# Whole or four-way split projections on TensorE: choosing the tile shape by the neighbouring pieces

## Chip, cores and metric

The kernel runs on one core of a Trainium2 chip. The metric is the device time of one execution in microseconds (us). The core has a matrix engine (TensorE, PE in the profile, with its weight loads shown apart as PEld), VectorE (DVE), ScalarE (ACT), GpSimd (POOL), and a queue on SyncE (SP) that issues most DMAs.

## The reference

One block of a recurrent model (RWKV) in float32, on 8 sequences of 256 tokens with 512 channels:

```python
xn = _ln(x, ln1_w, ln1_b); sx = _token_shift(xn, state[:, i1])
xxx = jnp.tanh((xn + sx * maa_x) @ maa_w1).reshape(b, l, 5, 1, 32)
xxx = jnp.matmul(xxx, maa_w2).reshape(b, l, 5, E)
x5 = xn[:, :, None] + sx[:, :, None] * (maa_stack + xxx)          # five mixes
w = jnp.exp(-jnp.exp(time_decay + jnp.tanh(x5[:, :, 1] @ decay_w1) @ decay_w2))
r, k, v = x5[:, :, 3] @ Wr.T, x5[:, :, 0] @ Wk.T, x5[:, :, 2] @ Wv.T
g = jax.nn.silu(x5[:, :, 4] @ Wg.T)
# scan over 256 steps, 32 heads of 16 channels:
#   a = k_t v_t;  out = r_t (u * a + s);  s = a + w_t * s
att = group_norm(outs) * gn_w + gn_b
x = x + att * g @ Wo.T
# feed-forward part: layer norm, token shift, two mixes, then
rr = jax.nn.sigmoid(xr @ ffn_Wr.T); kk = jnp.square(jax.nn.relu(xk @ ffn_Wk.T))
x = x + rr * (kk @ ffn_Wv.T)
```

## The kernel before

The work of one sequence is cut into pieces, each a few instructions of one engine, and into three stages: `inputs_of_scan` (layer norm, mixes, the projections to w, k, v, r, g), `scan` (the recurrence, as scans along time on VectorE over channel pairs, with sums on TensorE) and `rest` (group norm, output projection, feed-forward part). Stages of neighbouring sequences run at the same time.

The order is fixed before anything is emitted. `Plan.sequence` gives each piece a rank out of a long written table (`TURNS`). `Plan.order` then takes, again and again, the piece of lowest rank whose predecessors have been taken, and gives it a planned start from assumed costs (`LATENCY`, `SWITCH`, `GAP`, and the time in each piece). The order on each engine comes from the ranks, the dependencies and from which buffers are held. The planned times decide one more thing: which buffer of a pool a piece gets (the one freed last among those free at its planned start). On the chip each engine runs its pieces in that order and waits on semaphores.

The pieces of TensorE, with their lines:

- `project` (L576): 128 output channels of a projection, four contraction steps of a 128x128 weight tile against 256 tokens. `project_tokens` (L591): half a projection with tokens as the output rows, two steps against 512 channels. The same shape of work at L606, L701, L896 and, with 128 columns, L472. All of these use the whole 128x128 array; the planner calls that mode `full`.
- Transposes (L530), also on the whole array.
- Column pieces, which give each instruction 32 output columns, four of them side by side: `gather` (L793, sums of the scan, 16 matmuls), L735 and L819 (4 matmuls each). L658 (the decay and fifth-mix inputs) uses two tiles of 64 columns.
- Row pieces: L626 (32 rows), L673 and L834 (64 rows).

One matmul in float32 stands in the profile as two MATMUL instructions, each with its LDWEIGHTS. So a `project` piece is 8 MATMUL rows, a `project_tokens` piece 4, a `gather` 32.

Other lines that the text speaks of: L361 issues DMAs, L780 (multiply), L782 (scan) on VectorE and L785 on GpSimd are the recurrence, L648 and L859 are additions and products on GpSimd.

Of the kernel before, what the change touches and what calls it, by code (L numbers as in the profile page):

```python
# [58 lines left out]
class Op:  # L59
    def __init__(self, engine, us, outs, ins, emit, mode):  # L60
        self.engine, self.us, self.emit, self.mode = engine, us, emit, mode
        self.bufs = list(dict.fromkeys([*outs, *ins]))
        self.before, self.after, self.waits = [], [], 0
        self.ready = self.start = self.end = 0.0
        self.number, self.kind = 0, engine + "".join(c for c in self.bufs[0].name if not c.isdigit())


class Plan:
# [186 lines left out]
    def order(self, phases):  # L255
# [7 lines left out]
        while queue:  # L263
# [6 lines left out]
            at = max([at] + [sorted(s[0] for s in self.pools[p])[n - 1] for p, n in need.items()])  # L270
# [5 lines left out]
            if op.mode and op.mode != mode[op.engine]:  # L276
                at += self.SWITCH[op.engine]
                mode[op.engine] = op.mode
            for b in op.bufs:
# [18 lines left out]
            for o in op.after:  # L298
                same = o.engine == op.engine and op.lag < 1 and not op.wire
                o.ready = max(o.ready, op.end + self.GAP[op.engine] if same else landed + op.lag)  # L300
# [6 lines left out]
        self.span = max(op.end for op in done)  # L307
        return sorted(done, key=lambda op: op.start)


@with_exitstack
def tile_rwkv_block(
# [50 lines left out]

    def pe(us, outs, ins, emit, mode="full", into=()):
        plan.add("PE", us, outs, ins, emit, mode, into)

    def act(n, out, ins, emit, table=None, pointers=0):
        plan.add("ACT", 0.1 + n * 0.00084 + 0.09 * pointers, [out], ins, emit, table)

    def dve(n, outs, ins, emit, each=1.05):  # L370
        plan.add("DVE", 0.083 + n * each / 1e3, outs, ins, emit)

# [87 lines left out]
    def centered_weights():  # L460
# [5 lines left out]
        for k in range(NK):  # L466
            ps, w = new("ps", f"psW{k}"), wvs[k]
            for half in range(2):

                def mm(k=k, ps=ps, half=half):  # L470
                    for n in range(2):
                        nc.tensor.matmul(  # L472
                            ps()[:, half, n * P : (n + 1) * P], lhsT=raw[2 * half + n]()[:, k * P : (k + 1) * P],
                            rhs=cen()[:, 0, 0:P], start=True, stop=True)
# [10 lines left out]
    def normed(src, which, row, b, alone=False):  # L485
# [5 lines left out]
        if (which == 1 and b > 1) or (which == 2 and (b < 5)):  # L491
# [8 lines left out]
            gp(2, rs, [mv], lambda: nc.gpsimd.tensor_scalar(  # L500
                rs(), mv()[:, :, 1], 1.0 / E, EPS, ALU.mult, ALU.add), 30)
        else:
# [5 lines left out]
            act(2, mn, [mv], lambda: nc.scalar.mul(mn(), mv()[:, :, 0], -1.0))  # L508
            gp(2, rs, [mv, eh], lambda: nc.gpsimd.tensor_tensor(rs(), mv()[:, :, 1], eh()[:, 0:2], ALU.add), 30)
        gp(2, rs, [rs, eh], lambda: nc.gpsimd.tensor_tensor(rs(), rs(), eh()[:, 2:4], ALU.pow), 310)  # L510
        gp(2, nm, [mn, rs], lambda: nc.gpsimd.tensor_tensor(nm(), mn(), rs(), ALU.mult), 30)
        for n in range(NT):
# [7 lines left out]
            xh.append(t)  # L520
        xns, sxs = [], []
        i = NVEC + 2 * b + row
        for q in range(NQ):
# [7 lines left out]

            pe(0.55, [ps], [*xh, idt], turn, into=[xn])
            act(2, xn, [vec, ps], lambda q=q, xn=xn: nc.scalar.copy(xn()[:, :, 0:1], vec()[:, 2 * q : 2 * q + 2, i : i + 1]))
# [34 lines left out]
    def project(w, src, q, name, into):  # L568

        ps = new("ps", name)  # L570
        for m in range(2):
            o = (2 * q + m) * P

            def mm(m=m, o=o):
                for k in range(NK):
                    nc.tensor.matmul(  # L576
                        ps()[:, m, :], lhsT=w[k]()[:, o : o + P], rhs=src[k // 2]()[:, k % 2, :],
                        start=(k == 0), stop=(k == NK - 1),
                    )

            pe(1.73, [ps], [*w, *src], mm, into=[into])
        return ps

    def project_tokens(w, src, n, name, into):

        ps = new("ps", name)
        for h in range(2):

            def mm(h=h):
                for k in (2 * h, 2 * h + 1):  # L590
                    nc.tensor.matmul(  # L591
                        ps().rearrange("p m t -> p (m t)"), lhsT=src[h]()[:, k % 2, n * P : (n + 1) * P], rhs=w[k](),
                        start=(k == 0), stop=(k == NK - 1),
                    )

# [3 lines left out]
    def inputs_of_scan(b, got):  # L599
# [4 lines left out]
        def mm():  # L604
            for k in range(NK):
                nc.tensor.matmul(  # L606
                    px()[:, 0, :], lhsT=w1()[:, k, 0:P], rhs=xin[k // 2]()[:, k % 2, :], start=(k == 0), stop=(k == NK - 1))

        pe(1.73, [px], [w1, *xin], mm, into=[ta])
        act(256, ta, [px], lambda: nc.scalar.activation(ta(), px()[:, 0, :], AF.Tanh), "exp")  # L610

        def mixed(pair):
# [7 lines left out]
            for lot in lots:  # L620
# [9 lines left out]

                pe(0.97, [ps[g, q] for g, q, *_ in lot], [tb, w2b] if pair == (4,) else [ta, w2a], mm, "rows32", [x5[g][q] for g, q, *_ in lot])
                for g, q, *_ in lot:
# [28 lines left out]
        pe(1.73, [pd], [dw1, w1, *x5[1], *xin], mm, "columns64", [hd, tb])  # L661
        for rows in (slice(0, 64), slice(64, 128)):
# [12 lines left out]

        pe(0.97, pw, [dw2, hd], mm, "rows64", ws)
        for q in range(NQ):
# [14 lines left out]
        if b == 0:  # L692
# [3 lines left out]
            for m in range(2):  # L696
                ps, vo = new("ps", f"psv{b}_0_{m}"), new("vo", f"vo{b}_0_{m}")

                def mm(m=m, ps=ps):
                    for k in range(NK):  # L700
                        nc.tensor.matmul(  # L701
                            ps()[:, m, :], lhsT=vs_[k]()[:, m * P : (m + 1) * P], rhs=x5[2][k // 2]()[:, k % 2, :],
                            start=(k == 0), stop=(k == NK - 1))

                pe(1.73, [ps], [*vs_, *x5[2]], mm, into=[t])
                act(256, t, [ps], lambda m=m, t=t, ps=ps: nc.scalar.copy(t()[:, m, 1 : T + 1], ps()[:, m, :]))
# [13 lines left out]
    def scan(b, got):  # L720
# [17 lines left out]
        atts = [new("att", f"att{b}_{q}") for q in range(NQ)]  # L738
        pe(0.47, [pc], [hm, *rks], mm, "columns")
        for q in range(NQ):  # L740
# [4 lines left out]
        for blk in range(NK):  # L745
# [20 lines left out]
            for i in range(4):  # L766
# [9 lines left out]
                if i == 3 and ((b == 0 and blk) or (b == 1 and blk < 3)):  # L776
                    gp(4 * T, vs, [vs, k], lambda m=m, vs=vs, k=k: nc.gpsimd.tensor_tensor(
                        vs(), vs(), k.place[:, m : m + 1, 1 : T + 1].to_broadcast([P, 4, T]), ALU.mult))
                else:
# [3 lines left out]
                    st().rearrange("p n t -> p (n t)"), w().rearrange("p n t -> p (n t)"),  # L783
                    vs().rearrange("p n t -> p (n t)"), 0.0, ALU.mult, ALU.add), 2.06)
                gp(4 * T, st, [st, r], lambda m=m, st=st, r=r: nc.gpsimd.tensor_tensor(  # L785
                    st(), st(), r()[:, m : m + 1, :].to_broadcast([P, 4, T]), ALU.mult))
                done.append(st)
# [9 lines left out]

            pe(1.83, [pat], [con, *done], gather, "columns")
            dve(256, [att], [pat, att], lambda m=m, att=att, pat=pat: nc.vector.tensor_tensor(  # L799
# [5 lines left out]
    def rest(b, got):  # L805
# [16 lines left out]

        pe(0.47, [pv], [con, *sqs], mm, "columns")
        act(256, rs, [pv, eh], lambda: nc.scalar.activation(
            rs()[:, 0:T], pv()[:, 0, :], AF.Sqrt, bias=eh()[:, 0:1]), "sqrt", 1)
        dve(256, [rs], [rs], lambda: nc.vector.reciprocal(rs()[:, 0:T], rs()[:, 0:T]), 6.25)
        if last:
# [8 lines left out]

            pe(0.97, pr, [con, rs], mm, "rows64")
        ys = []
# [48 lines left out]
        for n in range(NT):  # L887
            o, t = os[n], x2[n]
            if last and n:
                for h in range(2):  # L890
# [3 lines left out]
                    def mm(ps=ps, n=n, cols=cols):  # L894
                        for k in range(NK):
                            nc.tensor.matmul(  # L896
                                ps()[:, 0, :], lhsT=kk[k // 2]()[:, k % 2, n * P : (n + 1) * P],
                                rhs=Wfv[k]()[:, cols], start=(k == 0), stop=(k == NK - 1))

# [20 lines left out]
    load(w2a, maa_w2[0:4].rearrange("g j e -> (g j) e"), 256)  # L920
    load(w2b, maa_w2[4:6].rearrange("g j e -> (g j) e"), 128)
    load(dw1, decay_w1.rearrange("(k p) j -> p k j", p=P), 128)
# [12 lines left out]
    with tc.manual_schedule():  # L935
        for op in plan.order(phases):
            op.emit()

# [73 lines left out]
```

## Time and profile before

| | us |
|---|---|
| Median of 3 runs (629.31 to 632.11) | 631.82 |
| The profiled execution | 631.53 |
| Its span, first to last instruction | 629.7 |
| TensorE busy, 3568 MATMULs | 608.1 |
| VectorE busy | 544.8 |
| GpSimd busy | 521.8 |
| ScalarE busy | 467.5 |

The profiled execution takes 1.8 us more than its span. The granted TensorE clock is 0.999 of full speed. Ends of matmuls are modelled in the profile, so the times between starts are what can be read closely: the duration of a row overlaps with the start of the next one.

### The profile page before, as it was taken

To read this page: it belongs to the slowest core of one execution; us is meant where nothing else is said; L and a number is where in the kernel's file an instruction comes from. 1 tells how busy PE (TensorE), PEld (TensorE's weight loads), DVE (VectorE), ACT (ScalarE), POOL (GpSimd) and SP (SyncE) were. 2 spreads that over 40 slices of the span, in tenths; PEclk is the share of its full clock that TensorE was granted. 3 is DMA by queue.
4 is the path that set the end of the run, shared out by engine and by line. 5 is a ranking of instruction groups with operands and counts; after the bars stand their busy time and mean duration, and the time that the engine had idled before them with its cause. 6 is when DMAs were issued, how large, how long until landed. Compare 5 with 4: busy or idle time off the path is not lost.

```text
span 629.7 us, 10253 instructions
## 1 busy us (share of the span) xinstructions
PE 608.1 (97%) x3568; PEld 408.6 (65%) x3568; DVE 544.8 (87%) x471; ACT 467.5 (74%) x1045; POOL 521.8 (83%) x420
## 2 busy tenths in 40 slices
PE   5899999999999999999999999999999999899997
PEld 4687777768555776477664776576765677556464
DVE  5689999999999999888997999899999999895331
ACT  2777869779977789788879798877887585776431
POOL 2699999899997999889888899999688989788040
PEclk9999999999999999999999999999999999999999
DMA  8697867597857877877778589598769886962541
GB/s 287 201 243 224 204 179 178 152 256 200 235 161 201 238 174 219 252 210 199 191 192 246 158 238 262 143 253 228 216 173 237 229 218 165 243 212 82 209 140 71
DMA packets 57778, 127.84 MB, mean 203 GB/s; under 512 B 7616, under 2 KB 16576, under 8 KB 57728
## 3 DMA queue, kind: packets, MB, share of 16 engines
q1 hardware_dynamic: 53360, 123.00, 72.3%
q10 hardware_dynamic: 4368, 4.20, 2.1%
q8 instruction: 28, 0.46, 0.3%
q14 instruction: 22, 0.18, 0.1%
HBM read 115.11 MB, written 8.39 MB: 196 GB/s over the span
## 4 chain that ended last, share of the span: by engine, by line
PE 64%; POOL 9%; DVE 8%; ACT 7%; DMA 6%; SPq 3%; issue 3%; ACTq 0%; POOLq 0%; DVEq 0%
PE ps L576 29%; PE ps L591 19%; PE ps L793 5%; DMA vs<-vo 5%; DVE st L782 4%; POOL st L785 4%; SPq L361 3%; PE ps L626 3%; PE ps L530 2%; PE ps L606 2%; PE ps L658 1%; POOL g L859 1%; DVE vs L780 1%; PE ps L673 1%; ACT xh L518 1%
## 5 line engine op out<-in xcount | busy, mean ns | idle before, releaser
L782 DVE TENSOR_TENSOR_SCAN st<-wrep,vs 128x1024 f32<-128x1024 f32 x128 | 289.4, 2279 | 6.3 <-ACT wrep L763 3.4
L785 POOL TENSOR_TENSOR st<-st,r 128x1024 f32<-128x1024 f32 x128 | 254.5, 2001 | 14.3 <-DVE st L782 13.8
L780 DVE TENSOR_TENSOR vs<-vs,ps 128x1024 f32<-128x1024 f32 x122 | 144.3, 1206 | 5.7 <-ACT vs L773 5.6
L591 PE MATMUL ps<-Ws,mix 128*128 128x512 f32 x248 | 112.3, 598 | 0.8 <-ACT o L883 0.8
L648 POOL TENSOR_TENSOR mix<-mix,xn 128x512 f32<-128x512 f32 x78 | 84.9, 1100 | 9.5 <-DVE mix L642 5.1
L591 PEld LDWEIGHTS ps<-Ws,mix 128*128 128x128 f32 x248 | 45.7, 190 | 53.3 <-issue 47.1
L636 ACT ACTIVATE ps<-ps,vec 128x256 f32<-128x256 f32 x140 | 59.5, 444 | 16.5 <-PE ps L626 14.6
L793 PE MATMUL ps<-st,con 128*32 128x256 f32 x1024 | 62.5, 382 | 0.9 <-POOL st L785 0.9
L576 PE MATMUL ps<-mix,Wr 128*128 128x256 f32 x256 | 60.7, 382 | 0.0
L576 PE MATMUL ps<-mix,Wg 128*128 128x256 f32 x256 | 60.7, 383 | 0.0
L576 PE MATMUL ps<-mix,Wk 128*128 128x256 f32 x256 | 60.3, 381 | 0.0
L591 PE MATMUL ps<-Ws,g 128*128 128x512 f32 x128 | 57.4, 599 | 2.8 <-POOL g L859 2.8
L576 PE MATMUL ps<-mix,Ws 128*128 128x256 f32 x256 | 59.3, 383 | 0.0
L576 PE MATMUL ps<-mix,Wv 128*128 128x256 f32 x240 | 56.6, 382 | 1.3 <-DVE att L799 0.9
L576 PEld LDWEIGHTS ps<-mix,Wg 128*128 128x128 f32 x256 | 47.6, 190 | 11.8 <-issue 5.0
L576 PEld LDWEIGHTS ps<-mix,Ws 128*128 128x128 f32 x256 | 47.7, 190 | 11.0 <-issue 3.8
L576 PEld LDWEIGHTS ps<-mix,Wk 128*128 128x128 f32 x256 | 47.8, 190 | 9.6 <-issue 3.4
L638 DVE TENSOR_TENSOR mix<-ps,sx 128x512 f32<-128x512 f32 x70 | 46.3, 680 | 8.9 <-ACT ps L636 7.6
L576 PEld LDWEIGHTS ps<-mix,Wr 128*128 128x128 f32 x256 | 47.5, 190 | 9.1 <-issue 1.7
L576 PEld LDWEIGHTS ps<-mix,Wv 128*128 128x128 f32 x240 | 44.9, 190 | 12.3 <-issue 3.1
L563 POOL TENSOR_TENSOR mix<-mix,xn 128x512 f32<-128x512 f32 x44 | 47.7, 1098 | 3.0 <-ACT mix L561 2.8
L773 ACT ACTIVATE vs<-s,cm 128x4 f32<-128x4 f32 x128 | 35.9, 295 | 18.5 <-DMA vs<-vo 17.2
(114 smaller groups left out, 902.7 us busy)
## 6 DMA issues: line engine op xcount, KB each, us to landing
vs<-vo SPq DMA_DIRECT2D x128, 512.0 KB, 5.5
Ws<-in_fr SPq DMA_DIRECT2D x16, 512.0 KB, 5.5
Ws<-in_wo SPq DMA_DIRECT2D x16, 512.0 KB, 4.9
Ws<-in_fk SPq DMA_DIRECT2D x16, 512.0 KB, 5.9
Ws<-in_fv SPq DMA_DIRECT2D x16, 512.0 KB, 4.6
x<-in_x SPq DMA_DIRECT2D x9, 512.0 KB, 5.6
vo<-v ACTq DMA_DIRECT2D x15, 256.0 KB, 2.7
out<-o SPq DMA_DIRECT2D x15, 256.0 KB, 3.7
```

What stands on the lines that cost most here:

```text
L361: plan.add("DMA", 0.6, [out] if out else [], [src] if src else [], lambda: nc.sync.dma_start(out=dst(), in_=in_()), lag=lag, kb=kb, part=part)
L563: gp(512, t, [t, xn[q]], lambda q=q, t=t: nc.gpsimd.tensor_tensor(t(), t(), xn[q]()[:, :, 1 : T + 1], ALU.add))
L576: nc.tensor.matmul(ps()[:, m, :], lhsT=w[k]()[:, o : o + P], rhs=src[k // 2]()[:, k % 2, :], start=(k == 0), stop=(k == NK - 1),)
L591: nc.tensor.matmul(ps().rearrange("p m t -> p (m t)"), lhsT=src[h]()[:, k % 2, n * P : (n + 1) * P], rhs=w[k](), start=(k == 0), stop=(k = ...
L636: act(256, p_, [p_, vec], lambda g=g, q=q, m=m, p_=p_: nc.scalar.activation(p_()[:, m, :], p_()[:, m, :], AF.Identity, bias=col(f"maa_{g}" ...
L638: dve(512, [t], [p_, sx[q]], lambda q=q, t=t, p_=p_: nc.vector.tensor_tensor(t(), p_(), sx[q](), ALU.mult))
L648: gp(512, t, [t, xn[q]], lambda q=q, t=t: nc.gpsimd.tensor_tensor(t(), t(), xn[q]()[:, :, 1 : T + 1], ALU.add))
L773: act(4, vs, [s0, cm], lambda i=i, blk=blk, vs=vs: nc.scalar.activation(vs()[:, :, 0:1], s0()[:, blk, 4 * i : 4 * i + 4].rearrange("p (n o ...
L780: dve(4 * T, [vs], [vs, kp], lambda m=m, vs=vs, kp=kp: nc.vector.tensor_tensor(vs(), vs(), kp()[:, m : m + 1, :].to_broadcast([P, 4, T]), ...
L782: dve(4 * T, [st], [w, vs], lambda w=w, vs=vs, st=st: nc.vector.tensor_tensor_scan(st().rearrange("p n t -> p (n t)"), w().rearrange("p n ...
L785: gp(4 * T, st, [st, r], lambda m=m, st=st, r=r: nc.gpsimd.tensor_tensor(st(), st(), r()[:, m : m + 1, :].to_broadcast([P, 4, T]), ALU.mult))
L793: nc.tensor.matmul(pat()[32 * i : 32 * i + 32, 0, :], lhsT=con()[:, s : s + 32], rhs=done[i]()[:, j, :], start=(j == 0), stop=(j == 3),)
```

## The change

A piece of TensorE that doesn't need a given shape now has the mode `any`. After the order is made, `Plan.tiles` walks TensorE's pieces and decides for each of them: behind a column piece it stays in columns, behind a transpose it stays whole; behind a row piece, or first of all, it looks ahead to the next piece with a mode of its own, and takes the whole array if that is a transpose and columns otherwise. In columns, `mul` issues four matmuls of 32 output columns in place of one of 128, with the same moving operand. L658 goes from two tiles of 64 columns to four of 32. The planner's costs are changed to match; `TURNS`, and so the order on each engine, is the same. (The array `maa_w2` and the slice of it are written in another way and hold the same.)

```diff
-    LATENCY = {"PE": 0.16, "DVE": 0.09, "ACT": 0.09, "POOL": 0.09, "DMA": 0.8}
-    SWITCH = {"ACT": 1.3, "PE": 0.1}
-    GAP = {"PE": 0.03, "DVE": 0.16, "ACT": 0.04, "POOL": 0.11, "DMA": 0.03}
+    LATENCY = {"PE": 0.12, "DVE": 0.09, "ACT": 0.09, "POOL": 0.09, "DMA": 0.8}
+    SWITCH = {"ACT": 1.3, "PE": 0.12}
+    AHEAD = {"PE": 0.2}
+    GAP = {"PE": 0.0, "DVE": 0.16, "ACT": 0.04, "POOL": 0.11, "DMA": 0.03}
...
+            ahead = self.AHEAD.get(op.engine, 0.0)
+            at = max([at] + [sorted(s[0] for s in self.pools[p])[n - 1] + ahead for p, n in need.items()])
...
+            want, now = op.mode, mode[op.engine]
+            if op.engine == "PE":
+                if want == "any":
+                    want = "any" if now in (None, "rows32", "rows64") else now
+                elif now == "any" and want in ("columns", "turn"):
+                    mode["PE"] = now = want
+            if want and want != now:
+                if now is not None or op.engine != "PE":
+                    at = max(at, free[op.engine] + self.SWITCH[op.engine])
+                mode[op.engine] = want
...
+    def tiles(self, ops):
+        mode = None
+        for n, op in enumerate(ops):
+            if op.mode != "any":
+                mode = op.mode
+            elif mode not in ("columns", "turn"):
+                mode = next((o.mode for o in ops[n:] if o.mode != "any"), "turn")
+                mode = "turn" if mode == "turn" else "columns"
+            op.narrow = mode == "columns"
...
+    def mul(out, w, x, first, final):
+        for i in range(0, P, 32) if narrow else (0,):
+            rows = slice(i, i + 32) if narrow else slice(0, P)
+            nc.tensor.matmul(out[rows], lhsT=w[:, rows], rhs=x, start=first, stop=final)
...
             def mm(m=m, o=o):
                 for k in range(NK):
-                    nc.tensor.matmul(
-                        ps()[:, m, :], lhsT=w[k]()[:, o : o + P], rhs=src[k // 2]()[:, k % 2, :],
-                        start=(k == 0), stop=(k == NK - 1),
-                    )
+                    mul(ps()[:, m, :], w[k]()[:, o : o + P], src[k // 2]()[:, k % 2, :], k == 0, k == NK - 1)
...
-                for rows, w, src in ((slice(0, 64), dw1()[:, k, :], x5[1]), (slice(64, 128), w1()[:, k, P : P + 2 * MAA], xin)):
+                for i in range(0, P, 32):
+                    w, src = (dw1()[:, k, i : i + 32], x5[1]) if i < DEC else (w1()[:, k, P + i - DEC : P + i - 32], xin)
                     nc.tensor.matmul(
-                        pd()[rows, 0, :], lhsT=w, rhs=src[k // 2]()[:, k % 2, :], start=(k == 0), stop=(k == NK - 1))
+                        pd()[i : i + 32, 0, :], lhsT=w, rhs=src[k // 2]()[:, k % 2, :], start=(k == 0), stop=(k == NK - 1))
```

`project_tokens` and the pieces at L472, L606, L701 and L896 call `mul` in the same way. The assumed times of many pieces are changed by some per cent (a gather from 1.83 to 1.735 us, a transpose from 0.55 to 0.45), those of short GpSimd instructions by more.

More of the change, by code (lines that the diff above doesn't have):

```diff
@@ L60, in __init__ @@
     def __init__(self, engine, us, outs, ins, emit, mode):
-        self.engine, self.us, self.emit, self.mode = engine, us, emit, mode
+        self.engine, self.us, self.emit, self.mode, self.narrow = engine, us, emit, mode, False
         self.bufs = list(dict.fromkeys([*outs, *ins]))
@@ L299, in order @@
                 same = o.engine == op.engine and op.lag < 1 and not op.wire
-                o.ready = max(o.ready, op.end + self.GAP[op.engine] if same else landed + op.lag)
+                o.ready = max(o.ready, op.end + self.GAP[op.engine] if same else landed + op.lag + self.AHEAD.get(o.engine, 0.0))
                 o.waits -= 1
@@ L307, in order @@
         self.span = max(op.end for op in done)
-        return sorted(done, key=lambda op: op.start)
+        done.sort(key=lambda op: op.start)
+        self.tiles([op for op in done if op.engine == "PE"])
+        return done
+    def tiles(self, ops):
[7 more added lines that the diff above has]
+            op.narrow = mode == "columns"
 @with_exitstack
@@ L370, in dve @@
     def dve(n, outs, ins, emit, each=1.05):
-        plan.add("DVE", 0.083 + n * each / 1e3, outs, ins, emit)
+        plan.add("DVE", 0.065 + n * each / 1e3, outs, ins, emit)
     def gp(n, out, ins, emit, each=1.86):
@@ L471, in mm @@
                     for n in range(2):
-                        nc.tensor.matmul(
-                            ps()[:, half, n * P : (n + 1) * P], lhsT=raw[2 * half + n]()[:, k * P : (k + 1) * P],
-                            rhs=cen()[:, 0, 0:P], start=True, stop=True)
+                        mul(ps()[:, half, n * P : (n + 1) * P], raw[2 * half + n]()[:, k * P : (k + 1) * P],
+                            cen()[:, 0, 0:P], True, True)
                 pe(0.46, [ps], [cen, *raw[2 * half : 2 * half + 2]], mm, into=[w])
@@ L520, in normed, with turned @@
             xh.append(t)
+        return turned(xh, which, row, b, alone)
+    def turned(xh, which, row, b, alone):
+        u = f"{which}_{b}"
         xns, sxs = [], []
@@ L590, in mm @@
                 for k in (2 * h, 2 * h + 1):
[L591 to L594, printed above, removed]
+                    mul(ps().rearrange("p m t -> p (m t)"), src[h]()[:, k % 2, n * P : (n + 1) * P], w[k](), k == 0, k == NK - 1)
             pe(1.72, [ps], [*src, *w], mm, into=[into])
@@ L605, in mm @@
             for k in range(NK):
-                nc.tensor.matmul(
-                    px()[:, 0, :], lhsT=w1()[:, k, 0:P], rhs=xin[k // 2]()[:, k % 2, :], start=(k == 0), stop=(k == NK - 1))
-        pe(1.73, [px], [w1, *xin], mm, into=[ta])
+                mul(px()[:, 0, :], w1()[:, k, 0:P], xin[k // 2]()[:, k % 2, :], k == 0, k == NK - 1)
+        pe(1.728, [px], [w1, *xin], mm, into=[ta])
         act(256, ta, [px], lambda: nc.scalar.activation(ta(), px()[:, 0, :], AF.Tanh), "exp")
@@ L629, in mm @@
                             )
-                pe(0.97, [ps[g, q] for g, q, *_ in lot], [tb, w2b] if pair == (4,) else [ta, w2a], mm, "rows32", [x5[g][q] for g, q, *_ in lot])
+                pe(0.945, [ps[g, q] for g, q, *_ in lot], [tb, w2b] if pair == (4,) else [ta, w2a], mm, "rows32", [x5[g][q] for g, q, *_ in lot])
                 for g, q, *_ in lot:
@@ L700, in mm @@
                     for k in range(NK):
[L701 to L705, printed above, removed]
+                        mul(ps()[:, m, :], vs_[k]()[:, m * P : (m + 1) * P], x5[2][k // 2]()[:, k % 2, :], k == 0, k == NK - 1)
+                pe(1.728, [ps], [*vs_, *x5[2]], mm, into=[t])
                 act(256, t, [ps], lambda m=m, t=t, ps=ps: nc.scalar.copy(t()[:, m, 1 : T + 1], ps()[:, m, :]))
@@ L738, in scan @@
         atts = [new("att", f"att{b}_{q}") for q in range(NQ)]
-        pe(0.47, [pc], [hm, *rks], mm, "columns")
+        pe(0.437, [pc], [hm, *rks], mm, "columns")
         for q in range(NQ):
@@ L796, in gather @@
                         )
-            pe(1.83, [pat], [con, *done], gather, "columns")
+            pe(1.735, [pat], [con, *done], gather, "columns")
             dve(256, [att], [pat, att], lambda m=m, att=att, pat=pat: nc.vector.tensor_tensor(
@@ L821, in mm @@
                     start=True, stop=True)
-        pe(0.47, [pv], [con, *sqs], mm, "columns")
+        pe(0.437, [pv], [con, *sqs], mm, "columns")
         act(256, rs, [pv, eh], lambda: nc.scalar.activation(
@@ L895, in mm @@
                         for k in range(NK):
-                            nc.tensor.matmul(
-                                ps()[:, 0, :], lhsT=kk[k // 2]()[:, k % 2, n * P : (n + 1) * P],
-                                rhs=Wfv[k]()[:, cols], start=(k == 0), stop=(k == NK - 1))
+                            mul(ps()[:, 0, :], kk[k // 2]()[:, k % 2, n * P : (n + 1) * P], Wfv[k]()[:, cols], k == 0, k == NK - 1)
                     pe(1.72, [ps], [*kk, *Wfv], mm, into=[y])
@@ L936, in tile_rwkv_block @@
         for op in plan.order(phases):
+            narrow = op.narrow
             op.emit()
```

34 lines of the change are left out of this document (15 added, 19 removed).

## The prediction

> **What bounds the kernel now.** I read the page first: busy times and the chain that ended last.
>
> ```profile
> span 629.7 us, 10253 instructions
> ...
> PE 608.1 (97%) x3568; PEld 408.6 (65%) x3568; DVE 544.8 (87%) x471; ACT 467.5 (74%) x1045; POOL 521.8 (83%) x420
> ...
> PE 64%; POOL 9%; DVE 8%; ACT 7%; DMA 6%; SPq 3%; issue 3%; ACTq 0%; POOLq 0%; DVEq 0%
> ```
>
> TensorE is busy 97% of the span and carries 64% of the chain. The rest of the chain goes through POOL, DVE, ACT and DMA, so not every microsecond that TensorE saves is one of the span.
>
> Next come the groups by line and shape, to see what the two shapes of matmul cost.
>
> ```profile
> L782 DVE TENSOR_TENSOR_SCAN st<-wrep,vs 128x1024 f32<-128x1024 f32 x128 | 289.4, 2279 | 6.3 <-ACT wrep L763 3.4
> L785 POOL TENSOR_TENSOR st<-st,r 128x1024 f32<-128x1024 f32 x128 | 254.5, 2001 | 14.3 <-DVE st L782 13.8
> ...
> L576 PE MATMUL ps<-mix,Wr 128*128 128x256 f32 x256 | 60.7, 382 | 0.0
> L793 PE MATMUL ps<-st,con 128*32 128x256 f32 x1024 | 62.5, 382 | 0.9 <-POOL st L785 0.9
> ...
> L576 PEld LDWEIGHTS ps<-mix,Wk 128*128 128x128 f32 x256 | 47.8, 190 | 9.6 <-issue 3.4 <-DVE st L782 0.2
> L793 PEld LDWEIGHTS ps<-st,con 128*32 128x32 f32 x1024 | 31.2, 109 | 27.5 <-issue 6.5 <-POOL st L785 2.5 <-POOL att L749 1.1
> ```
>
> 1024 matmuls of 32 columns (the gathers) keep TensorE busy for 62.5 us, 256 of 128 columns for 60.7: four narrow ones side by side pass in about the time of one whole one. A narrow weight load takes 109 ns, a whole one 190. The first two rows are the recurrence on the other full engines, kept here to see later whether they get slower.
>
> Third, TensorE's timeline, for what stands between pieces. In these rows the first number is the start; I use differences of starts.
>
> ```profile
> 301.85 0.60 PE L530 MATMUL ps<-idt,xh 128*128 128x128 f32 x4
> 302.29 1.89 PE L576 MATMUL ps<-mix,Wr 128*128 128x256 f32 x8
> 304.11 1.93 PE L793 MATMUL ps<-st,con 128*32 128x256 f32 x32
> 305.98 1.99 PE L576 MATMUL ps<-mix,Wg 128*128 128x256 f32 x8
> 307.90 0.64 PE L819 MATMUL ps<-sq,con 128*32 128x256 f32 x8
> ...
> 319.76 5.34 PE L576 MATMUL ps<-mix,Ws 128*128 128x256 f32 x24
> 324.94 1.89 PE L606 MATMUL ps<-mix,mw 128*128 128x256 f32 x8
> 326.76 1.93 PE L793 MATMUL ps<-st,con 128*32 128x256 f32 x32
> 328.63 1.15 PE L626 MATMUL ps<-ta,mw2a 32*128 32x256 f32 x16
> ```
>
> Three whole pieces in a row take 324.94 - 319.76 = 5.18 us, 1.727 us a piece or 0.216 us a step (a step is one whole MATMUL, or four narrow ones). A whole piece with a gather behind it takes 304.11 - 302.29 = 1.82; the gather, also 8 steps, 305.98 - 304.11 = 1.87; the whole piece between two column pieces 307.90 - 305.98 = 1.92. The work is the same 1.727 each time; what is added is a change of shape. Nothing else was late there: no row of these has an idle time with a releaser.
>
> **Part 1: the price of one change of shape.** The second steps of three pieces, from small windows of the timeline (in the PEld row, the loads for the next group begin with the second group):
>
> ```profile
> 304.35 0.13 PEld L793 LDWEIGHTS ps<-st,con 128*32 128x32 f32 x4
> ...
> 306.30 0.38 PE L576 MATMUL ps<-mix,Wg 128*128 128x256 f32 x1
> ...
> 328.95 0.39 PE L626 MATMUL ps<-ta,mw2a 32*128 32x256 f32 x4
> ```
>
> Entering columns: 304.35 - 304.11 = 0.24, which is 0.024 over a step. Entering the whole array: 306.30 - 305.98 = 0.32, 0.104 over. Entering rows: 328.95 - 328.63 = 0.32, 0.104 over. The first weight load stands open there, and the narrow one is the shorter. Leaving the whole array: 1.82 - 1.727 = 0.093. Leaving columns: 1.87 - 1.727 - 0.024 = 0.119, to the whole array (305.98) and to rows (328.63) alike.
>
> So a visit to the whole array costs 0.093 + 0.104 = 0.197 us, and a visit to columns 0.119 + 0.024 = 0.143. Row pieces stay what they are, and I count their ends as unchanged.
>
> **Part 2: how many changes go.** I walked TensorE's timeline from its first row to its last, 3568 MATMULs, and applied the rule of `tiles` to the pieces in this order, which the change keeps, as ranks and dependencies alone make it.
>
> ```profile
> 6.71 1.20 PE L472 MATMUL ps<-Ws,Ws 128*128 128x128 f32 x4 [6.71 <-DMA Ws<-in_wv]
> ...
> 624.08 1.89 PE L896 MATMUL ps<-Ws,mix 128*128 128x256 f32 x8
> ```
>
> Before, there are 138 changes of shape: 57 visits to the whole array, 48 to columns (7 of these only between 64 and 32 columns), 33 to rows. After, 85: 16 visits to the whole array, 36 to columns, 33 to rows. What goes is 41 visits to the whole array, 41 x 0.197 = 8.1 us, and 12 to columns, 12 x 0.143 = 1.7 us: 9.8 us of TensorE's time. About half of what is left stands around the row pieces.
>
> **Part 3: what is added.** By the same walk 103 pieces of 8 steps and 72 of 4 steps (plus two short ones at L472) become narrow, 1120 MATMULs, each of them four: 3360 more MATMULs, 128 more at L658, and as many loads. I cost a narrow step at a whole one's 0.216: the gather's 1.87 holds 8 steps and its two ends (0.143) and nothing more. For L591 no narrow step of 512 is in the trace; its bounds are the whole step and the same excess that a narrow 256 step shows (none), and I take zero. Two things are not in the trace: four tiles that read the same moving operand (the gather's four read different ones), and narrow work for long. The cover for all added loads is the step before them.
>
> [...] In the trace the four loads at 304.35 start inside the gather's matmuls of 304.11 to 306.04, and take 0.13 us without lengthening a step. [...]
>
> The loads and matmuls must also be brought to the engine and fetched as code:
>
> ```profile
> 485.21 0.64 PE L735 MATMUL ps<-rk,hm 128*32 128x256 f32 x8
> 485.67 1.91 PE L793 MATMUL ps<-st,con 128*32 128x256 f32 x32
> 487.51 1.98 PE L591 MATMUL ps<-Ws,g 128*128 128x512 f32 x4
> ...
> q8 instruction: 28, 0.46, 0.3%
> ```
>
> Two column pieces pass 40 MATMULs and 40 loads in 487.51 - 485.21 = 2.30 us: ten steps of 0.216 and the ends (2.16 + 0.14). That is the density of a narrow `project` piece, but only for 2.3 us; by the walk the longest narrow stretch after the change lasts 47 us, from 515 to 562. The code queue moves 0.46 MB, 64 bytes for each of the 7136 MATMULs and loads; they become 14,112, so it would be 0.9 MB in some 56 packets, on a queue whose share is 0.3%. I cost both at zero; the upper bound is in the rivals.
>
> **Part 4: what of it reaches the end.** 64% of the chain is TensorE's, and the changes of shape that go are spread over the span: 0.64 x 9.8 = 6.3 us lie on the path that sets the end now. The gain can't be more than that on this path; another path, now a little shorter, can become the longest. Where that is likeliest:
>
> ```profile
> 40.00:100.00 60.00, 59.55 (x415) 45.48 (x417) 58.74 (x49) 45.10 (x104) 59.54 (x41) 1.00 0.82 212
> ...
> 300.00:400.00 100.00, 100.00 (x590) 65.33 (x592) 91.22 (x72) 84.19 (x192) 90.76 (x74) 1.00 0.79 210
> ```
>
> The columns are length, busy PE, PEld, DVE, ACT, POOL, clock, DMA share and rate. From 300 to 400 TensorE is full and DVE and POOL have 9 us each to spare: what is saved there counts. From 40 to 100 POOL (59.54) and DVE (58.74) are as full as TensorE; 1.2 us of the 9.8 lie there by the walk, and POOL leaves 0.46. I take off 0.8: 6.3 - 0.8 = 5.5 us.
>
> The profiled execution is 631.53 us, 0.3 below the median of the three runs. 631.5 - 5.5 = 626.0 us. The most that the sum allows, with all 9.8 on the path, is 621.7.
>
> **Rivals.** *The gain is hidden.* Where the chain goes through POOL and DMA (36% of it is not TensorE's), TensorE arrives earlier and waits longer. The planned starts move too, so pieces get other buffers of the same pools, and a buffer may come free later than the one before.
>
> ```profile
> PE ps L591 <- POOL g L859: 2.8, 3, 1.5
> ```
>
> That is the largest group of waits of TensorE in mid-run, three of them, 1.5 us at the longest. Two more like the longest, with a bit lost in each stretch, would leave some 2 us of 5.5: 629.5 us. For it: DVE 87% and POOL 83% busy, and an order that was written for other lengths of pieces. Against it: 100 of 100 us of TensorE from 300 to 400.
>
> *Slower: narrow work in long stretches isn't fed.* The place is the 103 narrow pieces of 8 steps, with 64 instructions each instead of 16; those of 4 steps have half the density. The point from which it decides: 9.8 / 103 = 0.095 us a piece, that is 1.82 us in place of 1.727. The price by the nearest dearer row, the gather's 1.87: 0.14 x 103 = 14.7 us, less 9.8 is 4.9 us of TensorE. A slower TensorE is paid nearly in full, as it has no room: 634.5 (64%) to 636.4. The same sum holds if four readers of one operand cost something. Against it: the 2.30 us above at full density, and the unlengthened gathers. For it: no row shows more than that.
>
> [...]
>
> *It doesn't do what it says*: the choice leaves most pieces whole. The walk gives 177 narrow pieces of 272, so this would need the order to be another: 631.5.
>
> **How the numbers follow.** What a measurement of this kernel can tell from no change is about 0.5%, 3.2 us: faster means under 628.4, slower over 635.0 on the scale of 631.5-631.8. Forecast (5.5 us, with its own range from 621.7 to 628.3): 0.68. Hidden gain: 0.18. Little or no effect, with the choice going otherwise: 0.03. Not fed, or dearer steps: 0.08, of which a part ends within 0.5%; sequencer rule 0.02; overlap rule 0.01. Faster 0.68, same 0.22, slower 0.10. The range starts at 621.5 and, to take in the hidden gain and a narrow step that is dearer by a little, ends at 632.5.
>
> **What would show it.** Right: MATMULs go from 3568 to about 7056; narrow L576 pieces stand 1.73 us apart in a row; changes of shape drop from 138 to 85; the share of TensorE on the chain falls a little and waits of TensorE for POOL or DVE rise; the code queue doubles. Wrong: a narrow piece above 1.82 us, idle times of PEld put down to "issue" growing within pieces, L782 or L785 longer than their 2279 and 2001 ns, or the same steps with new waits of TensorE adding up to more than 4 us.

## The result: the changed kernel is 1.0% slower

The changed kernel takes 637.40 us (median of 4 runs, 636.73 to 639.55) against 631.76 for the kernel before. The ratio is 1.0104, 95% interval 1.0069 to 1.0138. The forecast was 626.0, its range ended at 632.5, and the sign is wrong too. The profiled execution took 639.55 us, with a span of 637.7. Of the runs below, one execution of e5 and one of e6 took 3.59 ms and are left out of their ratios.

From its page, the lines that answer to those of before (L393 is `mul`, L805 and L808 are the scan and the product that were L782 and L785, L796 was L773, L816 is the gather that was L793, L382 issues DMAs):

```profile
span 637.7 us, 17228 instructions
PE 606.4 (95%) x7056; PEld 363.4 (57%) x7056; DVE 545.1 (85%) x471; ACT 467.4 (73%) x1045; POOL 521.9 (82%) x420
q8 instruction: 55, 0.90, 0.6%
PE 38%; DMA 17%; POOL 14%; DVE 12%; ACT 10%; issue 4%; SPq 4%; ACTq 0%; POOLq 0%; DVEq 0%
PE ps L393 30%; DMA vs<-vo 13%; DVE st L805 6%; POOL st L808 6%; SPq L382 4%; PE ps L816 3%; PE ps L650 2%; DVE vs L803 2%; POOL mix L594 2%; POOL sx L575 1%; DMA sq<-sq 1%; PE ps L561 1%; ACT ps L660 1%; DVE mix L662 1%; POOL mix L672 1%
L805 DVE TENSOR_TENSOR_SCAN st<-wrep,vs 128x1024 f32<-128x1024 f32 x128 | 289.3, 2278 | 8.2 <-ACT wrep L786 3.7
L808 POOL TENSOR_TENSOR st<-st,r 128x1024 f32<-128x1024 f32 x128 | 254.5, 2001 | 14.4 <-DVE st L805 13.1
```

The instructions did what was said: 7056 MATMULs, the code queue up from 0.46 to 0.90 MB, the recurrence as fast as before (2278 and 2001 ns). But TensorE fell from 64% of the chain to 38%, and what took its place first of all is DMA, from 6% to 17%. TensorE's timeline shows that narrow pieces in a row aren't the cause:

```profile
526.23 1.91 PE L393 MATMUL ps<-mix,Wv 128*32 128x256 f32 x32
527.96 1.91 PE L393 MATMUL ps<-mix,Wr 128*32 128x256 f32 x32
529.69 1.91 PE L393 MATMUL ps<-mix,Wg 128*32 128x256 f32 x32
```

They start 1.73 us apart, 0.216 a step, as costed. The waits changed. First two groups of before, then the same two of after (total us, times, longest), then TensorE's longest new ones of after:

```profile
ACT vs L773 <- DMA vs<-vo: 17.2, 18, 2.3
POOL att L850 <- DMA sq<-sq: 3.3, 2, 2.5
```

```profile
ACT vs L796 <- DMA vs<-vo: 29.1, 28, 2.6
POOL att L873 <- DMA sq<-sq: 9.5, 3, 4.8
PE ps L816 <- POOL st L808: 2.8, 1, 2.8
PE ps L758 <- ACT g L741: 2.4, 1, 2.4
```

ScalarE and GpSimd wait longer for data (`vs` is the operand of the scan, broadcast by DMA; `sq` is read back for the group norm), and then TensorE waits for them: its idle times of more than 0.15 us add up to 27.1 us, against 17.8 before. So transfers come later: from issue to landing `vs` takes 6.0 us in the median, before 5.5. The question of the runs was why: the change adds no data transfer and its order on every engine is that of before.

### The profile page after: what moved, and what is told of

It reads as the page before. It is cut to its first block, busy times and chain, and to the rows that moved or that the text cites. A ratio compares the mean times of both kernels' runs of the same rounds, so it can differ in the third digit from the quotient of the medians.

```text
span 637.7 us, 17228 instructions
## 1 busy us (share of the span) xinstructions
PE 606.4 (95%) x7056; PEld 363.4 (57%) x7056; DVE 545.1 (85%) x471; ACT 467.4 (73%) x1045; POOL 521.9 (82%) x420
## 4 chain that ended last, share of the span: by engine, by line
PE 38%; DMA 17%; POOL 14%; DVE 12%; ACT 10%; issue 4%; SPq 4%; ACTq 0%; POOLq 0%; DVEq 0%
PE ps L393 30%; DMA vs<-vo 13%; DVE st L805 6%; POOL st L808 6%; SPq L382 4%; PE ps L816 3%; PE ps L650 2%; DVE vs L803 2%; POOL mix L594 2%; POOL sx L575 1%; DMA sq<-sq 1%; PE ps L561 1%; ACT ps L660 1%; DVE mix L662 1%; POOL mix L672 1%
## 5 line engine op out<-in xcount | busy, mean ns | idle before, releaser
L805 DVE TENSOR_TENSOR_SCAN st<-wrep,vs 128x1024 f32<-128x1024 f32 x128 | 289.3, 2278 | 8.2 <-ACT wrep L786 3.7
L808 POOL TENSOR_TENSOR st<-st,r 128x1024 f32<-128x1024 f32 x128 | 254.5, 2001 | 14.4 <-DVE st L805 13.1
L393 PE MATMUL ps<-Ws,mix 128*32 128x512 f32 (+1 forms) x792 | 115.8, 589 | 1.7 <-ACT o L906 0.8
L393 PEld LDWEIGHTS ps<-Ws,mix 128*32 128x32 f32 (+1 forms) x792 | 40.2, 119 | 62.5 <-issue 51.8
L816 PE MATMUL ps<-st,con 128*32 128x256 f32 x1024 | 65.3, 388 | 3.2 <-POOL st L808 2.8
L393 PE MATMUL ps<-mix,Wv 128*32 128x256 f32 (+1 forms) x736 | 60.7, 380 | 3.2 <-DVE mix L662 1.1
L393 PE MATMUL ps<-mix,Wk 128*32 128x256 f32 (+1 forms) x664 | 61.3, 380 | 0.0
L393 PE MATMUL ps<-Ws,g 128*32 128x512 f32 (+1 forms) x464 | 59.0, 604 | 2.0 <-POOL g L882 2.0
L393 PE MATMUL ps<-mix,Wr 128*32 128x256 f32 (+1 forms) x688 | 60.6, 380 | 0.0
L393 PE MATMUL ps<-mix,Wg 128*32 128x256 f32 (+1 forms) x856 | 60.4, 379 | 0.0
L393 PE MATMUL ps<-mix,Ws 128*32 128x256 f32 (+1 forms) x712 | 59.2, 379 | 0.1
L796 ACT ACTIVATE vs<-s,cm 128x4 f32<-128x4 f32 x128 | 36.4, 297 | 30.8 <-DMA vs<-vo 29.1
L393 PEld LDWEIGHTS ps<-mix,Wv 128*32 128x32 f32 (+1 forms) x736 | 41.7, 120 | 19.9 <-issue 2.6
L816 PEld LDWEIGHTS ps<-st,con 128*32 128x32 f32 x1024 | 35.7, 111 | 27.4 <-POOL st L808 5.5
L393 PEld LDWEIGHTS ps<-mix,Wk 128*32 128x32 f32 (+1 forms) x664 | 42.6, 124 | 14.4 <-issue 1.7
L393 PEld LDWEIGHTS ps<-mix,Ws 128*32 128x32 f32 (+1 forms) x712 | 40.1, 122 | 17.0 <-ACT mix L592 1.1
L766 ACT COPY att<-ps 32x256 f32<-32x256 f32 x128 | 46.5, 363 | 3.1 <-POOL g L882 0.9
```

What stands on the lines that cost most here:

```text
L393: nc.tensor.matmul(out[rows], lhsT=w[:, rows], rhs=x, start=first, stop=final)
L766: act(350, atts[q], [pc], lambda i=32 * (2 * q + m), m=m, q=q, h=32 * h: nc.scalar.copy(atts[q]()[h : h + 32, m, :], pc()[i : i + 32, 0, :]))
L796: act(4, vs, [s0, cm], lambda i=i, blk=blk, vs=vs: nc.scalar.activation(vs()[:, :, 0:1], s0()[:, blk, 4 * i : 4 * i + 4].rearrange("p (n o ...
L805: dve(4 * T, [st], [w, vs], lambda w=w, vs=vs, st=st: nc.vector.tensor_tensor_scan(st().rearrange("p n t -> p (n t)"), w().rearrange("p n ...
L816: nc.tensor.matmul(pat()[32 * i : 32 * i + 32, 0, :], lhsT=con()[:, s : s + 32], rhs=done[i]()[:, j, :], start=(j == 0), stop=(j == 3),)
```

## The experiments

Three theories. A: the new planner costs give pieces other buffers, some of which come free later. B: narrow instructions themselves cost, on TensorE or its sequencer. C: TensorE's code, now 55 packets of 16 KB in place of 28, gets in the way of the data transfers. From e5 on, the expectations call B, as the rival of C, theory D. Each run is compared with the kernel before on the same chip.

**One half of the change at a time.** e1 has the changed planner and all its buffers, but every piece whole (and L658 as two tiles):

```diff
-            op.narrow = mode == "columns"
+            op.narrow = False
```

> The changed planner costs, and so the changed buffers, with every projection issued whole and the decay piece as two tiles of 64 columns, as before. Theory A (the new buffers cost the time, the narrow issue saves some 5 us): the narrow saving is gone and the buffers' loss stays, 640 to 645 us, slower than the kernel before by 1.5 to 2%. Theory B (the narrow issue itself costs the time; the buffers are neutral): 630 to 633 us, the same as before.

e2 has the planner and buffers of before, and only issues narrow:

```diff
+        plan.stages[-1][-1].issue = issue or {"full": "any", "columns64": "columns"}.get(mode, mode)
...
+            op.narrow = mode == "columns"
```

> The old planner costs and so the old buffers, with the projections issued narrow or whole by the changed rule and the decay piece as four tiles of 32 columns. Theory A: 624 to 628 us, faster than before by about 1%. Theory B: 636 to 640 us, like the changed kernel. In both 85 changes of shape and 7056 MATMULs.

e1: 631.26 us, ratio 0.9995 (0.9974 to 1.0017). e2: 638.67, 1.0097 (1.0065 to 1.0129). The whole loss is in the narrow issue; theory A falls. Two more runs took the buffer freed first in place of last, after (e3) and before (e4):

```diff
-                    b.slot = max((s for s in self.pools[b.pool] if s[0] <= at), key=lambda s: s[0])
+                    b.slot = min(self.pools[b.pool], key=lambda s: s[0])
```

> The changed kernel, but each piece takes the buffer of its pool that came free first, in place of the one that came free last; the order on each engine stays. Theory A: waits for buffers shrink, as the time between two uses of a buffer is the longest that the order allows; clearly under 637, 625 to 632 us. Theory B: 636 to 640 us.

> The kernel before with the same choice of the buffer that came free first. Theory A: 628 to 635 us, and the kernel e3 below it by some 5 us, as only the issue and a few buffers differ between the two. Theory B: about the same as before, 630 to 633, and e3 above it by 6 us.

e3: 1.0094 (1.0057 to 1.0131), e4: 1.0022 (0.9999 to 1.0045). Buffers don't decide it.

**Code without narrow tiles.** e5 adds NoOps on TensorE to the whole pieces of before (6 behind each matmul of `project`, 14 behind each of `project_tokens`), for about as much code as the change makes:

```diff
+                    idle(6)
...
+                    idle(14)
```

> The kernel before, all pieces whole, with 6424 instructions added on TensorE's queue that do nothing (6 behind each matmul of 256, 14 behind each of 512), so that its code is nearly as long as the changed kernel's (some 53 code packets in place of 28) with no narrow matmul in it. Theory C (the longer code is what costs: its fetches delay the data's DMAs): the DMAs land later, 5.5 us on the mean in place of 5.1, and the time is 635 to 641 us. Theory D (the narrow matmuls themselves cost): the landings stay at 5.1 and the time at 630 to 633 us. If the added instructions hold TensorE up, its steps would stand over 0.216 us apart, and the run says nothing.

659.9 us, 1.0421 (1.0367 to 1.0474). Its page shows that this is another effect:

```profile
PE 636.9 (97%) x3568; PEld 388.8 (59%) x3568; DVE 547.2 (83%) x471; ACT 467.9 (71%) x1045; POOL 521.8 (79%) x420
```

TensorE is 28.8 us longer busy: steps of 512 columns, with 14 NoOps behind each, start 0.504 us apart in place of 0.429 (those of 256 stay at 0.216). The run says nothing on C. e9 does it without work on TensorE: the code of before is spread over more blocks of 256 instructions. Empty space is put between pieces, and one branch at the end of each block jumps over it (10,315 instructions in its profile, 62 more than before).

```diff
+            if op.engine == "PE":
+                n = 32 if op.mode == "columns64" else size[op.us]
+                if since + n > 128:
+                    nc.tensor.addr_align(256, max_nops=0)
+                    since = 0
+                since += n
```

> The kernel before, with TensorE's code moved on to the next block of 256 instructions after at most 128 of them (62 times; the rest of a block is jumped over and not executed). The matmuls, their order and the buffers are those of the kernel before; the code packets become 60 to 64 in place of 28, a little more than the changed kernel's 55. Theory C (each code packet stops the data's DMAs for a while): DVE, POOL and PE arrive later by steps of 0.5 to 2 us, the data rate dips at each packet, and the time is 636 to 645 us with no narrow matmul in it. Theory D (the narrow matmuls themselves cost): 630 to 634 us. A stop of TensorE at each jump would show as gaps between its steps at the places of the jumps.

642.42 us, 1.0156 (1.0127 to 1.0186): slower than the changed kernel, with all tiles whole. From its page:

```profile
PE 612.3 (95%) x3568; PEld 410.1 (64%) x3568; DVE 546.2 (85%) x471; ACT 468.4 (73%) x1045; POOL 522.1 (81%) x420
q8 instruction: 62, 1.02, 0.7%
PE 50%; DMA 15%; DVE 12%; POOL 9%; ACT 8%; issue 3%; SPq 2%; ACTq 0%; DVEq 0%; POOLq 0%
L773 ACT ACTIVATE vs<-s,cm 128x4 f32<-128x4 f32 x128 | 36.5, 297 | 35.2 <-DMA vs<-vo 33.8
```

The same picture as the changed kernel's: DMA 15% of the chain, `vs` late by 33.8 us in all, TensorE idle for 26.7 us. No idle time of its matmuls over 0.15 us is put down to "issue", neither here nor in the changed kernel: these 26.7 and 27.1 us are put down to other engines and to data. Theory C makes the picture; narrow tiles (B) aren't needed for it.

What happens at a packet can be seen at one place. In e9 a code packet starts at 260.10 us. First SyncE's timeline (start, us), then windows of 1 us (the last two columns are DMA share and GB/s), of e9:

```profile
260.33 1.56 SPq L361 DMA_DIRECT2D vs<-vo  x1
...
259.00:260.00 1.00, 1.00 (x4) 0.45 (x3) 1.00 (x1) 0.97 (x3) 0.00 (x0) 1.00 0.15 39
260.00:261.00 1.00, 1.00 (x3) 0.38 (x2) 1.00 (x1) 0.34 (x2) 0.62 (x1) 1.00 0.52 92
261.00:262.00 1.00, 1.00 (x4) 0.50 (x3) 1.00 (x3) 0.50 (x1) 1.00 (x2) 1.00 0.99 358
```

And the same transfer of before, where no packet is near:

```profile
256.77 0.56 SPq L361 DMA_DIRECT2D vs<-vo  x1
...
256.00:257.00 1.00, 1.00 (x4) 0.52 (x3) 1.00 (x1) 1.00 (x3) 0.11 (x1) 1.00 0.29 40
257.00:258.00 1.00, 1.00 (x4) 0.42 (x3) 1.00 (x2) 0.03 (x1) 1.00 (x2) 1.00 0.88 332
```

Issuing takes 1.56 us in place of 0.56, and the transfer lands 8.4 us after the start of its issue in place of 6.2. The two sets of windows lie differently to the issue; counted from its start, in quarters of a microsecond, the rate is 98, 98, 180 and 352 GB/s in e9 and 90, 131 and 401 before, so it comes up only a quarter of a microsecond later. Where the rest of the 2.2 us goes isn't shown.

In the changed kernel's trace 17 issues of SyncE after the first 20 us last over 0.7 us, where 0.54 is usual, and all 17 lie within 1 us of a code packet; they add 11.2 us. Of the other 54 issues that lie as near to a packet none is over 0.7 us, so a packet nearby doesn't always make a long issue. In the trace of before 7 are that long, with 4.5 us.

Averaged over the changed kernel's packets, in windows of 0.2 us, the data rate is 220 GB/s one microsecond before a packet's start, 126 to 143 in the first microsecond behind it, and 185 some 1.6 us after it. The fall begins some 0.8 us ahead of the packet, so this average alone doesn't tell cause from effect; that added packets cost time is shown by e9. Not each packet comes with a fall: at one place where a long transfer was already running (e9 at 65.73 us: 236 GB/s in the microsecond before its start, 222 and 231 in the two behind it) the rate stays.

**Room for the transfers.** If C is right, the loss goes when transfers have time. e6 and e7 load, from the third sequence on, a sixteenth of each streamed weight (the rest of the weight tiles is left as it was), before and after:

```diff
+                dma(t, lambda h=h: src[2 * h * P : (2 * h + 2) * P, 0:32].rearrange("(k p) e -> p k e", p=P),
+                    lambda t=t: t()[:, :, 0:32], 524)
```

> The kernel before with less DMA work: from the third sequence on, only 32 of the 512 columns of the streamed weights Wo and of the feed-forward part are loaded, so what is computed with them isn't the reference's. Both theories: some us faster than before, 618 to 630; it is the yardstick of the next.

> The changed kernel with the same part of the weights left out (from the third sequence on, 32 of 512 columns loaded). Theory C: with the data's DMAs no longer late, the saved changes of shape show: 3 to 8 us under e6. Theory D: 4 to 8 us above e6, as the changed kernel is above the one before.

e6: 631.18 us, slower than expected, 0.9969 (0.9941 to 0.9996), e7: 1.0046 (1.0021 to 1.0071). The gap shrinks little, from 1.0 to 0.8%; the weights weren't the transfers that were late. q1, the data queue, still moved most of its bytes in e7:

```profile
q1 hardware_dynamic: 53360, 99.41, 62.0%
```

e10 and e11 load a sixteenth of the scan's operand as well (its broadcast `vs<-vo`, from the third sequence on), before and after:

```diff
+                wide = 4 * T if b < 2 else T // 4
```

> The kernel before with little DMA work from the third sequence on: 32 of 512 columns of the streamed weights, and 64 of 1024 elements of the scan's broadcast operand, are loaded, so most of the output isn't the reference's. Both theories: 610 to 628 us, TensorE on most of the chain. It is the yardstick of the next.

> The changed kernel with the same loads left thin. Theory C: with the DMAs short, a stop of theirs is covered, and most of the 9.8 us of changes of shape comes through: 4 to 9 us under e10. Theory D: the loss of the narrow work stays, 3 to 8 us above e10.

And e13 is e10 with the padding of e9:

> The thin-stream kernel of e10 (weights and scan operands loaded in part only, so these inputs are not the reference's) with whole tiles and TensorE's code stretched by padding as in e9, to some 62 code packets in place of 28. If a packet costs by holding up data transfers that are late, the thin transfers cover it: 625 to 629 us, within 0.4% of e10's 626.8. If a packet costs TensorE or the issuing queues themselves, whatever the data traffic, the 34 packets cost as much as in e9 (10 us): 634 to 639 us.

The data queue and the chain of e10, of e11, and code queue and chain of e13:

```profile
q1 hardware_dynamic: 53360, 52.22, 30.4%
PE 83%; POOL 5%; ACT 3%; DMA 3%; DVE 2%; SPq 2%; issue 1%; POOLq 0%; DVEq 0%; ACTq 0%
```

```profile
PE 64%; POOL 11%; DVE 9%; ACT 5%; DMA 5%; issue 3%; SPq 2%; ACTq 0%; POOLq 0%; DVEq 0%
```

```profile
q8 instruction: 62, 1.02, 0.7%
PE 75%; DMA 7%; POOL 6%; DVE 5%; ACT 4%; issue 2%; SPq 1%; ACTq 0%; DVEq 0%; POOLq 0%
```

e10: 0.9933 (0.9910 to 0.9957). e11: 0.9906 (0.9891 to 0.9922): the narrow kernel no longer loses, its ratio is 0.27% lower, 1.7 us, though the intervals overlap. That is less than was expected of it. e13: 0.9953 (0.9934 to 0.9971), 0.2% above e10, which the intervals don't part from nothing, where the same padding cost 1.56% on full transfers. TensorE is busy for 607.5 us in e13 and 607.3 in e10, so neither the code nor the branches lengthen its own work: the 62 packets cost through transfers that have no time to spare. In e13's trace 14 issues are still over 0.7 us, 10.1 us in all, and hardly move the end.

**Number or places of the packets?** Two kernels go narrow only in short runs (at most 24, or 12, steps) that touch a column piece and no transpose:

```diff
+                    op.narrow = "turn" not in ends and "columns" in ends and steps <= self.LIMIT
```

> The changed kernel, but projections become narrow only where a column piece stands at one end or both of a run of them, no transpose at the other, and the run has at most 24 steps: by the walk 4.9 us of changes of shape go, for 1824 added instructions (7 code packets) in place of 6976 (27). Theory C, with 13 us of loss over 27 packets, 0.47 a packet: 0.64 x 4.9 = 3.1 saved, 3.3 lost, 630 to 633 us. Theory D, with a loss for all narrow work in proportion (456 of 1744 float32 matmuls added, against 840 x 2 before): 631 to 635 us. The two are close here; the run says mainly whether part of the saving can be had.

> As e8, but only runs of at most 12 steps become narrow: some 2 us of changes of shape go, for 312 added instructions at them and 256 at L683, 2 code packets. Theory C: 1.2 us saved, 1 lost, 630 to 632 us, within the noise of e8. Theory D: 630 to 632 us as well; the run places e8's gain, if it has one, between limits.

e8, with 36 packets: 630.11 us, 0.9975 (0.9949 to 1.0001). e12, with 30: 634.31, 1.0037 (1.0019 to 1.0055). Fewer packets and slower, against C in its plain form. The next five move the whole code by part of a block, so that as many packets meet other transfers; e14 (before), e15 (e8) and e16 (after) by half a block, e18 (after) by a quarter, and e17 begins the padding of e9 half a stretch earlier:

```diff
+        nc.tensor.addr_align(256, offset=128, max_nops=0)
```

> The kernel before with the whole code of TensorE moved by 128 instructions (half a block), so the same 28 code packets fall elsewhere between the transfers; nothing else differs. If the places of the packets matter, it stands 1 to 5 us off the kernel before, to either side (627 to 637 us); if only their number matters, within 0.3%: 630 to 633.5 us.

> The kernel of e8 (narrow only in short runs, limit 24) with the same half-block shift of TensorE's code; same number of code packets as e8. If places matter, 1 to 5 us off e8's 630.1 (most likely above, as e12 was); if only the number matters, 629 to 632 us.

> The changed kernel with TensorE's code moved by 128 instructions. Same 56 code packets, other places. If the number sets the loss and places only scatter it (as e14 and e15 did, by 0.3% and 0.7%): 0.4% to 1.7% above the kernel before, 634 to 643 us. If the loss was an accident of places: as likely below the kernel before as above it, 624 to 634 us.

> The changed kernel with TensorE's code moved by 64 instructions, a third sample of places. Number: 0.4% to 1.7% above the kernel before, 634 to 643 us. Accident of places: 624 to 634 us as likely as not.

> The padded kernel of e9 (whole tiles, some 62 code packets) with its padding placed half a stretch earlier, so that the packets fall between those of e9. Number: again 1.0% to 2.1% above the kernel before, 638 to 646 us. Accident of places: within 0.5% of it, 629 to 635 us.

| code packets | ratio to before, one number for each kernel |
|---|---|
| 28 | 1 (before), 0.9995 (e1), 1.0022 (e4), 1.0033 (e14) |
| 30 | 1.0037 (e12) |
| 36 | 0.9975 (e8), 1.0044 (e15) |
| 55 or 56 | 1.0097 (e2), 1.0104 (after), 1.0094 (e3), 1.0118 (e16), 1.0137 (e18) |
| 62 | 1.0156 (e9), 1.0158 (e17) |

The intervals of the last five runs: e14 1.0009 to 1.0056, e15 1.0024 to 1.0065, e16 1.0083 to 1.0154, e18 1.0106 to 1.0168, e17 1.0126 to 1.0190. Both are at work. The places scatter a kernel by up to 0.7% (e8 and e15, the same instructions), which takes in e12. The number carries the loss: all seven kernels with 55 packets or more are 0.9% or more above the kernel before, at every place that was tried. e8 is the best with the full computation, but its interval reaches 1 and the shift undid its gain: no version that beats the kernel before is shown.

## Why the prediction was wrong, step by step

*The price of a change of shape* (Part 1) and *their number* (Part 2) were right. By the same walk of the changed trace there are 85 changes, and each takes what it took before, for instance 0.217 us more than its steps from columns to the whole array (0.119 + 0.104 predicted). So the 9.8 us are saved on TensorE's work, before its waits.

*The cost of the narrow steps* (Part 3) was right: 1.73 us a piece. The rival "not fed" falls. No run shows what the chances call "sequencer rule" and "overlap rule" (0.02 and 0.01); what the runs showed in their place is the 1.73 us, and a TensorE that was busy for 606.4 us with 7056 MATMULs against 608.1 with 3568.

*The code* (Part 3: "so it would be 0.9 MB in some 56 packets, on a queue whose share is 0.3%. I cost both at zero") is the step that failed. The count was right, 55 packets; the price was read off the share of the queue. The 55 packets' own time is 0.6% of the queues'. A packet cost by what it held up: 34 packets more make 1.57% in e9 and e17, 9.9 us, 0.29 us each. For the change's 27 that is an estimate of 7.9 us, more than the whole forecast gain. I had put no range on it: the upper bound that Part 3 points to in the rivals is one for narrow work that isn't fed, and no row of the trace showed that a packet is free. The row that could have warned me was there: in the trace of before, six of SyncE's seven long issues (0.80 to 1.57 us where 0.54 is usual) lie within 1 us of a code packet.

*What reaches the end* (Part 4) was mis-sized as well. 64% of 9.8, less 0.8, was to give 5.5 us. With transfers out of the way the difference is 1.7 us (e11 to e10), and an estimate of 2.7 us if 27/34 of the 1.3 that e13 shows for its packets is added back: 28% of 9.8 in place of 56%. TensorE is busy for 6.6 us less there (600.7 against 607.3), but its idle times of more than 0.15 us grow by 4.5 us (18.3 against 13.8). The share of an engine on the chain says what holds the end now, not what a shorter engine gives back: in e11 TensorE falls from 83% to 64% of the chain, POOL and DVE rise from 7% together to 20%. That the rest is lost mainly to those two is argued from the chain; no run shortened them. The rival "the gain is hidden" had named this, at 629.5, and it holds where code costs nothing; it is only half of what happened.

The sum of the two, 7.9 lost and 1.7 to 2.7 gained, is 5.2 to 6.2 us slower; measured is 6.6 (4.4 to 8.7). Each of the two estimates is known to some 2 us only, so that they come this near is partly luck. The warning sign in the prediction, "new waits of TensorE adding up to more than 4 us", is what came: the 2.8 and 2.4 us above alone are 5.2.

What stays open: how a code packet holds an issue on SyncE, and how much of its price is that, how much a lower rate of transfers that are running, and how much the half clock that was recorded at TensorE's waits of 2.8 and 2.4 us (last section). No run parts the three.

## What to carry to other kernels

Splitting instructions wasn't free here, though the engine had room for them (1.73 us a narrow piece, as costed): the code queue went from 0.46 to 0.90 MB, and a block more cost 0.29 us where the kernel waited for transfers (e9, e17). So count blocks, and price them by padding the old code before the new is written. Of the time saved on the busiest engine an estimated 28% reached the end, where the forecast, from its share of the chain, had 56%; look what is next late. And where a kernel is this full, move the code by half a block before believing a difference of half a percent: here that moved e8 by 0.7%.

## What the runs showed of the hardware

*What a code packet cost.* TensorE's code came in packets of 16,384 bytes: 55 for 14,112 MATMULs and loads, and 28 for 7136 before, which is 257 and 255 of them a packet and an estimate of some 64 bytes each. A packet cost 0.29 us where transfers were late (e9, e17); where they had room it was some 0.04 (1.3 us for 34 in e13), not clear of nothing.

*The clock after a wait.* In the changed kernel's profile, windows around the wait of 2.8 us (length, then busy PE, PEld, DVE, ACT and POOL, then the granted clock, DMA share and GB/s):

```profile
263.00:266.90 3.90, 1.05 (x21) 0.68 (x24) 1.38 (x2) 3.83 (x11) 3.90 (x4) 1.00 1.03 312
266.90:270.30 3.40, 3.40 (x29) 1.48 (x22) 1.86 (x3) 2.44 (x4) 3.40 (x4) 0.52 1.05 273
270.30:273.70 3.40, 3.40 (x36) 1.76 (x32) 3.27 (x3) 3.27 (x9) 3.40 (x4) 0.98 1.07 336
```

TensorE was busy for 1.05 of 3.90 us, and then ran at half clock for 3.413 us by the records of the clock, from 267.04 us on. There were two such stretches in mid-run, the other from 492.32 us at the wait of 2.4 us and also of 3.413 us; an estimate from their length is up to 1.7 us of TensorE each. They aren't the whole loss: two other runs of the changed kernel had a granted clock of 1.000 and took 636.73 and 637.47 us. But in e3 and e7 a lower clock went with a longer run: in e3 the three runs at 0.999 or more took 634.20 to 635.90 us, the four at 0.994 to 0.997 took 638.89 to 641.30, and of e7's twelve runs the two at 1.000 took 632.6, the other ten 635.2 on the mean. How much of this is the half clock and how much the long wait ahead of it isn't parted.
